# Two attention layers on one core: v in quarter products within the stream of q, k and projection

## The chip, the core and the metric

The kernel runs on one NeuronCore of a Trainium2 chip. Its time is the time of one execution on the device in microseconds (us), taken as the median of several runs. A profile of one further execution shows when each engine was busy and what it waited for. The engines are TensorE (PE, its weight loads are listed as PEld), VectorE (DVE), ScalarE (ACT), GpSimd (POOL) and SyncE (SP), which issues most transfers.

## The reference

Two layers of the same form are applied to x of 8 images, 512 channels and 32 x 32 positions, all in float32. They differ in the groups of the normalisation (8 and 32).

```python
xn = group_norm(x) * scale + bias                # (B, 512, 1024)
q, k, v = split(qkv_w @ xn + qkv_b)              # 8 heads of 64 channels each
attn = softmax(q^T k / 8)                        # (B, 8, 1024, 1024)
out = proj_w @ (v attn^T) + proj_b + x
```

## The kernel before

The work is cut into 16 units, one for each layer and image (`units`, L103). A unit has two stages on TensorE: the products of v, q and k, with the projection of the unit before it, and then the attention. All engines run the order that is written out in the code; waits between them are semaphores.

**Products by Strassen's scheme.** Every 512 x 512 by 512 x 1024 product is made of seven half-size products in Winograd's form. The weights' mixtures are made once, kept in DRAM as images (`store_image`, `load_image`, L186 to L194) and loaded for each unit. The mixtures of the activations are made in each unit by subtractions: class `Right` (L196) has `mix` (L215) for the outer level and `quarter` (L221) for the inner one. q, k and the projection use two levels: 7 x 7 parts. v uses one level.

**The stream** (`Stream`, L396). `product` (L407) makes one outer product of seven inner parts, one matmul with 256 columns each (L417), in the order 1, 6, 2, 7, 5, 4, 3 (`ORDER`, L50). Part 1 goes to `one`, a corner of one PSUM pair (`sbank`), and ACT copies it (`seed`, L422) to a quarter of another pair (`apair`), where later parts add to it; part 6 is then added to `one`, and so on. The seventh part goes to a corner of its own and is copied to `late` (L434). The last two parts, 4 and 3, stand in `tail` and run after part 1 of the following product, so that the copies of ACT lie beside matmuls. `finish` reads the finished pair with DVE (`sum_steps`, L456, and its users), and POOL adds `late` (`add_late`, L452). Consecutive products use the two pairs `apair` in turn. `hook` calls after each product what `at` has put there: pieces of other work in the order in which the engines shall do them.

**v** (`make_values`, L606). Each of the seven outer products is eight matmuls of 256 columns (L394), with the activations as weights, so that v comes out with positions on partitions. ACT copies two results, DVE adds five. In this time POOL makes the inner factors of x for q and k (`make_rooms`, `part_of`, L935 to L955, shown as L947), in rooms that lie in the tiles of k, of p and of tmp.

**The attention** (`attention`, L693). It has 64 steps, in 8 chunks of 8. A step makes scores (L718) in a PSUM pair, ACT takes the exponential into a tile p (L726; there are five such buffers), TensorE multiplies it with v (L746), and DVE adds p to a running sum (`summed`, L763 and L765). At the end of a chunk the result is evacuated (`evacuate`, L767: ACT copies one bank to tmp, DVE adds the other, L772), the sums are transposed and reduced (L777, L785), and some steps later `reciprocals` and `divide` (L796, L823) finish a pair of heads. `at_step` (L1081) puts the next unit's work in between: normalisation, two mixtures of x (L1116, by L217), loads of weights. The last pair's `reciprocals`, `divide` and `bias_last` are done in the next unit's hooks (L1017 to L1019), and the factors of its projection are made there by DVE (`o_rooms`, L1003, shown as L1015).

## Time and profile before

| what | value |
|---|---|
| median of 3 runs | 3210.49 us (3210.27 to 3212.94) |
| profiled execution | 3212.51 us |
| its span in the profile | 3210.7 us |
| granted TensorE clock | 0.999 |
| busy: PE, DVE, ACT, POOL | 3195.5, 2773.0, 1892.3, 930.4 us |
| one period: attention of unit 13; v, then q, k and projection, of unit 14 | 110.26; 24.71; 63.50 us |
| matmul records of v, L394, 128 x 256 (mean of one) | 382 ns |
| matmul records of the stream, L417, 128 x 256 | 379 to 386 ns |

The span runs from the first to the last instruction of the profile; the execution's own time has 1.8 us more around it. Busy times of an engine are of its instructions, and an idle engine costs nothing unless another waits for it. A matmul's record lasts longer than the step to the next one, because matmuls are pipelined: what counts is the distance from start to start. A float32 matmul gives two records. In the rows of the timeline, the first number is the start and the second the length in us; rows of like instructions in succession are merged, with their number at the end.

### The profile page before, as it was taken

The numbers are of one execution on the slowest core, as the hardware profiler recorded it, in microseconds if no ns is written. First come the engines' busy times: TensorE is split into PE (matmuls) and PEld (weight loads), VectorE is DVE, ScalarE is ACT, GpSimd is POOL, SyncE is SP. The second block draws the span as 40 slices with busy tenths as digits, with TensorE's granted clock in tenths as the row PEclk, the third lists the DMA queues.
The fourth block names the chain that finished last, engine by engine and source line by source line (L and its number), as shares of the span: only waits on it lengthen the run. The fifth ranks groups of instructions, "written<-read, shape, count | busy, mean of one in ns | idle before, by whom it ended". The sixth has DMA issues, their size and how long they took to land.

```text
span 3210.7 us, 59813 instructions
## 1 busy us (share of the span) xinstructions
PE 3195.5 (100%) x23012; PEld 2023.7 (63%) x23012; DVE 2773.0 (86%) x3315; ACT 1892.3 (59%) x3077; POOL 930.4 (29%) x619
## 2 busy tenths in 40 slices
PE   9999999999999999999999999999999999999999
PEld 7466584765847658476584755747557485674843
DVE  7988988989899898888988889898888988989877
ACT  3656746466465665746657465574655746557464
POOL 5133060330604306043150421504224042240520
PEclk9999999999999999999999999999999999999999
DMA  5334242442534314233142332423323233232311
GB/s 197 109 108 131 79 159 96 132 131 93 160 105 128 120 45 157 74 108 127 43 162 68 107 124 61 143 70 122 108 79 126 74 119 106 86 130 74 123 64 49
DMA packets 151361, 344.84 MB, mean 107 GB/s; under 512 B 27168, under 2 KB 40992, under 8 KB 151072
## 3 DMA queue, kind: packets, MB, share of 16 engines
q1 hardware_dynamic: 150784, 340.81, 33.2%
q8 instruction: 187, 3.06, 0.4%
q14 instruction: 102, 0.84, 0.1%
q10 hardware_dynamic: 288, 0.13, 0.0%
HBM read 282.29 MB, written 57.02 MB: 106 GB/s over the span
## 4 chain that ended last, share of the span: by engine, by line
PE 94%; DVE 3%; issue 1%; POOL 0%; ACT 0%; DMA 0%; SPq 0%; DVEq 0%; POOLq 0%; ACTq 0%
PE a L746 26%; PE s L718 25%; PE s L417 18%; PE a L417 13%; PE a L394 6%; PE s L394 5%; DVE acc L765 1%; PE a L718 1%; PE s L672 0%; PE a L672 0%; DVE tr L777 0%; DVE acc L763 0%; DVE red L785 0%; DVE ao L772 0%; DVE xt L217 0%
## 5 line engine op out<-in xcount | busy, mean ns | idle before, releaser
L726 ACT ACTIVATE p<-s 128x1024 f32<-128x1024 f32 x976 | 997.6, 1024 | 522.7 <-PE s L718 495.4
L746 PE MATMUL a<-p,v 64*64 64x512 f32 x8192 | 1102.3, 589 | 0.0
L718 PE MATMUL s<-q,k 64*64 64x512 f32 x7808 | 1060.8, 590 | 0.0
L765 DVE TENSOR_TENSOR acc<-acc,p 128x1024 f32<-128x1024 f32 x768 | 938.3, 1222 | 77.9 <-ACT p L726 34.6
L746 PEld LDWEIGHTS a<-p,v 64*64 64x64 f32 x8192 | 385.1, 132 | 494.2 <-ACT p L726 348.3
L718 PEld LDWEIGHTS s<-q,k 64*64 64x64 f32 x7808 | 388.1, 133 | 426.9 <-issue 426.9
L422 ACT COPY a<-s 128x256 f32<-128x256 f32 x1308 | 465.8, 357 | 282.3 <-PE s L417 202.4
L947 POOL TENSOR_TENSOR k<-xn 128x512 f32<-128x512 f32 x16 | 20.3, 1269 | 1337.0 <-DVE xn L217 1337.0
L434 ACT COPY late<-s 128x256 f32<-128x256 f32 x327 | 121.7, 372 | 179.9 <-PE s L417 178.8
L394 PE MATMUL a<-w,xn 128*128 128x256 f32 x768 | 178.2, 382 | 0.5 <-DVE v L623 0.5
L832 ACT ACTIVATE ao<-ao,vec 128x512 f32<-128x512 f32 x128 | 88.4, 715 | 143.9 <-DVE ao L825 143.7
L394 PEld LDWEIGHTS a<-w,xn 128*128 128x128 f32 x768 | 144.6, 190 | 31.8 <-issue 12.2
L763 DVE TENSOR_TENSOR acc<-p,p 128x1024 f32<-128x1024 f32 x128 | 152.5, 1192 | 9.4 <-ACT p L726 9.4
L777 DVE STREAM_TRANSPOSE tr<-acc 128x1024 f32<-128x1024 f32 x128 | 158.0, 1235 | 0.0
L785 DVE TENSOR_REDUCE red<-tr 128x32 f32<-128x1024 f32 x128 | 154.3, 1206 | 0.6
L417 PE MATMUL s<-xn,w 128*128 128x256 f32 x492 | 146.8, 380 | 1.2 <-POOL xn L947 1.2
L417 PE MATMUL s<-k,w 128*128 128x256 f32 x492 | 146.4, 379 | 0.0
L417 PE MATMUL a<-xn,w 128*128 128x256 f32 x492 | 146.4, 379 | 0.0
L772 DVE TENSOR_TENSOR ao<-a,tmp 128x512 f32<-128x512 f32 x128 | 88.1, 688 | 61.4 <-ACT tmp L771 61.2
L417 PE MATMUL a<-xt,w 128*128 128x256 f32 x462 | 137.5, 379 | 0.0
L288 POOL TENSOR_TENSOR y<-var,half 128x4 f32<-128x4 f32 (+1 forms) x17 | 22.8, 1340 | 381.7 <-DVE var L286 381.7
L417 PE MATMUL s<-xt,w 128*128 128x256 f32 x432 | 128.5, 379 | 0.0
(204 smaller groups left out, 4685.9 us busy)
## 6 DMA issues: line engine op xcount, KB each, us to landing
w<-iq SPq DMA_DIRECT2D x105, 448.0 KB, 3.4
w<-ik SPq DMA_DIRECT2D x105, 448.0 KB, 5.8
w<-io SPq DMA_DIRECT2D x105, 448.0 KB, 3.4
rb<-drec SPq DMA_DIRECT2D x128, 256.0 KB, 3.9
w<-iv SPq DMA_DIRECT2D x105, 256.0 KB, 2.8
xn<-mid SPq DMA_DIRECT2D x36, 512.0 KB, 3.5
xn<-x_dram SPq DMA_DIRECT2D x32, 512.0 KB, 4.3
res<-x_dram SPq DMA_DIRECT2D x32, 512.0 KB, 6.5
```

Source lines behind the costliest of these rows:

```text
L394: step()
L417: nc.tensor.matmul(dst, a[j], b[j], start=start, stop=j != 1, skip_group_check=True),
L422: n = nc.scalar.copy(dst, one)
L434: on("ACT", nc.scalar.copy(late, seventh), s, 1)
L718: nc.tensor.matmul(bank[e * H : (e + 1) * H, j, :], w.k[pr][j * H : (j + 1) * H, t * P + e * H : t * P + (e + 1) * H], w.q[pr][j * H : (j ...
L726: exp = nc.scalar.activation(p, bank, AF.Exp, scale=SCALE)
L746: nc.tensor.matmul(banks[r][j * H : (j + 1) * H, :], w.v[rows, t, lo : lo + D], p[rows, j, :], start=(t == 0), stop=(t == NT - 1),)
L763: nc.vector.tensor_add(acc, state["first"], p)
L765: nc.vector.tensor_add(acc, acc, p)
L777: nc.vector.transpose(tr, state["acc"].pop(c))
L785: nc.vector.tensor_reduce(red[:, :, qh, :], state["tr"].rearrange("p j (f i) -> p j f i", i=BL), AX.X, ALU.add)
L832: nc.scalar.activation(cols, cols, AF.Identity, bias=vec[:, units[u][0], VB, pr : pr + 1])
```

## The change

v is now made in two levels, too, except in unit 0: `stream_values` runs seven stream products before those of q. A part of v is two matmuls of 128 columns, with 128 positions of the activations as weights; the image of v's weights therefore has the inner mixtures too (448 KB for a product instead of 256). The results of v are added by DVE (p1's first half is copied by ACT), and POOL adds `late` to them.

The inner factors of x have to be there when v begins. A new method, `single`, makes those of one outer factor. The factors of products 1 and 6 are made by DVE in the attention before (`mixing`, steps 44 to 60), in rooms of k's first tile, and the two outer mixtures that were at steps 50 and 59 are at 43 and 50. The factors of products 2 and 3 are made by POOL at the end of the attention (`begin_high`: four subtractions of 128 x 512, in the buffers of p that come free next); those of 5, 7 and 4 by POOL after them, in rooms of k.

At the end of the attention, the last chunk is evacuated by DVE alone, a copy and an addition, ahead of its last sum; its transposition and reduction, and the bias of the pair before, go to hooks in v. The reciprocals and the division move to the ends of v and of q's second product. Of the projection's factors, DVE makes those of products 1, 5, 6 and 7, POOL those of 2, 3 and 4. The pairs of PSUM banks swap their parts from unit to unit (`banks_of`), since the stream now has 28 products. The check of the sums is done once, at the end, on maxima and minima kept for each pair of heads.

```diff
+    q_pairs, k_pairs = (
+        [qkpool.tile([P, 2, N], F32, tag=f"{sel}{r}", name=f"{sel}{r}") for r in range(2)] for sel in "qk"
+    )
...
-        def quarter(self, pair, rooms, engine):
+        def quarter(self, pair, rooms, engine, kept=None):
             v = self.views[pair[0]]
             t1, t2, t4 = rooms
             b11, b12, b21, b22 = (v[:, :, c, q, :] for c in range(2) for q in range(2))
+            b7 = b12 if kept is None else kept
...
+        def single(self, k, rooms, engine, kept=None):
+
+            v, (t1, t2, t4) = self.outer[k], rooms
+            b11, b12, b21, b22 = (v[:, c, q * FD2 : (q + 1) * FD2] for c in range(2) for q in range(2))
+            b7 = b12 if kept is None else kept
+            self.inner[k] = {1: b11, 2: b21, 3: b22, 7: b7, 5: t1, 6: t2, 4: t4}
+            sub = engine.tensor_sub
+            return [
+                partial(sub, t1, b12, b11), partial(sub, t2, b22, t1), partial(sub, t4, b21, t2),
+                partial(sub, b7, b22, b12),
             ]
...
             def part(j, dst, tile_name, bank, start=False):
-                on(
-                    "PE",
-                    nc.tensor.matmul(dst, a[j], b[j], start=start, stop=j != 1, skip_group_check=True),
-                    tile_name, bank,
-                )
+                for to, at, moving in (
+                    [(dst[:, ts(i, P)], b[j][:, ts(i, P)], a[j]) for i in range(2)]
+                    if tokens else [(dst, a[j], b[j])]
+                ):
+                    on(
+                        "PE",
+                        nc.tensor.matmul(
+                            to, at, moving, start=start, stop=j != 1, skip_group_check=True
+                        ),
+                        tile_name, bank,
+                    )
+                    start = False
...
+        cols = to[:, 1].rearrange("p (a t) o -> p a t o", a=2)
+        parts = late.rearrange("p (t o) -> p t o", o=P)[:, None].to_broadcast([P, 2, 2, P])
+        return nc.gpsimd.tensor_add(cols, cols, parts)
...
+            if bias is None:
+                on("ACT", nc.scalar.copy(t[:, 0, :], main[:, 0, :]), m, 0)
+                on("DVE", nc.vector.tensor_add(in_two(t[:, 1, :]), in_two(main[:, 1, :]), twice(late)), m, 1)
+                return
...
+    def stream_values(stream, w, left, hook):
+        st, p1, u2, u3, wide = sum_steps(None, None, f"v_{w.u}")
+
+        def block(r, h):
+            return w.v[:, ts(h, NT // 2), ts(r, FD2)].rearrange("p t (r o) -> p r t o", o=P)
+
+        def result(r, h, more):
+            def finish(main, m, late):
+                to = block(r, h)
+                w.last["v"].append(
+                    on("DVE", nc.vector.tensor_add(to, by_rows(main), by_rows(st[more])), m, 0, 1)
+                )
+                w.last["v"].append(add_late_v(to, late))
+
+            return finish
+
+        def fifth(main, m, late):
+            to = block(1, 1)
+            for i in range(2):
+                wide(main, m, i)
+                w.last["v"].append(
+                    on(
+                        "DVE",
+                        nc.vector.tensor_add(to[:, i], by_rows(main)[:, i], by_rows(st["u3"])[:, i]),
+                        m, i,
+                    )
+                )
+            w.last["v"].append(add_late_v(to, late))
+
+        steps = {
+            1: p1, 6: u2, 2: result(0, 0, "p1"), 7: u3, 5: fifth, 4: result(1, 0, "u3"),
+            3: result(0, 1, "u2"),
+        }
+        for k in ORDER:
+
+            def finish(main, m, late, k=k):
+                steps[k](main, m, late)
+                hook("v", k)
+
+            stream.product(left.quarters(k), w.right.inner[k], k == 3, finish, True)
...
+        def banks_of(c):
+            pair = (c + g) % 2
+            return abank[2 * pair : 2 * pair + 2]
...
-            i0 = nc.scalar.copy(tmp, banks[0])
+            if c == n_chunks - 1 and not final:
+                i0 = nc.vector.tensor_copy(tmp, banks[0])
+            else:
+                i0 = nc.scalar.copy(tmp, banks[0])
...
-            summed(s, p)
+            if s < n_steps - 1:
+                summed(s, p)
             at_step(s, state)
         products(n_steps - 1)
         evacuate(n_chunks - 1)
-        for h in range(NH):
-            add_bias(CC - 2, h)
-        transposed(n_chunks - 1)
-        reduced(n_chunks - 1)
+        summed(n_steps - 1, p)
+        w.sums = [partial(transposed, n_chunks - 1), partial(reduced, n_chunks - 1)]
...
+            right.mix(3)
+            fifth = right.single(5, in_k((1, 1, 3), (1, 0, 0), (1, 0, 1)), nc.gpsimd)
+            run(fifth[:2])
+            run(right.single(7, in_k((1, 0, 2), (1, 0, 3), (1, 1, 2)), nc.gpsimd))
+            run(fifth[2:])
+            at("v", 6, partial(right.mix, 2), partial(run, right.single(4, in_k((1, 1, 0), (1, 1, 1), (0, 1, 3)), nc.gpsimd)))
...
+            def o_rooms(ro=ro, parts=o_parts):
+                ta, tb = (trpool.tile([P, 2, FD], F32, tag="tr", name=f"o{i}_{u}") for i in "ab")
+                oa, ob = (ppool.tile([P, 2, FD], F32, tag="p", name=f"o{i}_{u}") for i in "cd")
+                v, g = nc.vector, nc.gpsimd
+                parts[1] = ro.single(1, [alone(ta, *i) for i in ((0, 0), (0, 1), (1, 0))], v)
+                parts[7] = ro.single(7, [alone(ta, 1, 1), alone(tb, 0, 0), alone(tb, 1, 0)], v)
+                parts[5] = ro.quarter((5, 6), (halves(tb)[1], *halves(oa)), v)
+                parts[2] = ro.quarter((2, 3), (*halves(ob), halves(xt[:, 1])[0]), g)
+                rooms = alone(xt[:, 1], 0, 1), alone(xt[:, 1], 1, 1), alone(xt[:, 0], 0, 0)
+                parts[4] = ro.single(4, rooms, g)
+
+            def o_part(k, lo=0, hi=4):
+                return lambda: run(o_parts[k][lo:hi])
+
+            transposed, reduced = old.sums
+            at("v", 1, transposed)
+            at("v", 2, reduced)
+            at("v", 4, reciprocals, old.bias_before)
+            at("v", 3, partial(ro.mix, 0), o_rooms)
+            at("q", 1, o_part(1, 0, 2))
+            at("q", 6, divide)
+            at("q", 2, bias_last, o_part(1, 2))
+            at("q", 7, partial(ro.mix, 1))
+            at("q", 4, partial(ro.mix, 3))
+            at("q", 3, partial(ro.mix, 2))
+            at("k", 1, o_part(5, 0, 2))
+            at("k", 6, o_part(5, 2))
+            at("k", 2, o_part(7), o_part(2, 0, 2))
+            at("k", 7, o_part(2, 2))
+            at("k", 4, o_part(4))
+
+        stream = Stream((u + 1) % 2)
+        if u == 0:
+            stream.close(
+                make_values(w, lefts["v"], (apair[1], sbank[0], apair[0]), hook, between, behind)
+            )
+        else:
+            stream_values(stream, w, lefts["v"], hook)
...
+        mixing = {}
+        if not last:
+            first_1 = right.single(1, [alone(w.kp[0], *at) for at in ((0, 0), (0, 1), (1, 0))], nc.vector)
+            first_6 = right.single(
+                6, [alone(w.kp[0], *at) for at in ((1, 1), (0, 2), (1, 2))], nc.vector, alone(w.kp[0], 0, 3)
+            )
+            mixing.update(zip((44, 46, 47, 52), first_1))
+            mixing.update(zip((54, 55, 59, 60), first_6))
+            mixing[43] = partial(right.mix, 0)
+            mixing[50] = partial(right.mix, 1)
+
+            def begin_high(right=right):
+                xa, xb = (ppool.tile([P, 2, FD], F32, tag="p", name=f"x{i}_{u + 1}") for i in "ab")
+                run(right.quarter((2, 3), (*halves(xa), halves(xb)[0]), nc.gpsimd, halves(xb)[1]))
...
+            if s in mixing:
+                mixing[s]()
 
         stream.close()
         attention(w, at_step)
+        if not last:
+            begin_high()
```

## The prediction

> **What bounds the kernel now.** I read the engine totals first, then one late period by stage, then the order in time of each engine around the one seam that the change rebuilds.
>
> ```profile
> PE 3195.5 (100%) x23012; PEld 2023.7 (63%) x23012; DVE 2773.0 (86%) x3315; ACT 1892.3 (59%) x3077; POOL 930.4 (29%) x619
> ```
>
> TensorE is busy all the time. The stage windows of one period say that this is real. The rows are the attention of unit 13 (2669.97 to 2780.23), and of unit 14 v (to 2804.94) and q, k and projection (to 2868.44):
>
> ```profile
> 2669.97:2780.23 110.26, 110.26 (x1034) 49.96 (x1033) 98.90 (x123) 76.27 (x83) 4.10 (x4) 1.00 0.25 77
> 2780.23:2804.94 24.71, 24.71 (x117) 21.73 (x115) 20.00 (x21) 5.53 (x8) 17.38 (x12) 1.00 0.36 127
> 2804.94:2868.44 63.50, 63.48 (x294) 55.17 (x293) 53.50 (x61) 37.37 (x104) 37.00 (x25) 1.00 0.42 136
> ```
>
> The columns after the length are busy time of PE, weight loads, DVE, ACT and POOL. PE has no hole in 198.47 us. DVE is busy for 98.9 of 110.3 us of the attention, so it has little room there. The timeline of PE gives the pace of the matmuls; each float32 matmul is two records:
>
> ```profile
> 12.41 1.39 PE L330 MATMUL s<-gmat 128*128 128x128 f32 x11
> 2777.48 2.81 PE L746 MATMUL a<-p,v 64*64 64x512 f32 x24
> 2780.23 3.72 PE L394 MATMUL a<-w,xn 128*128 128x256 f32 x16
> 2810.12 0.59 PE L417 MATMUL a<-k,w 128*128 128x256 f32 x2
> 2810.55 0.60 PE L417 MATMUL a<-xt,w 128*128 128x256 f32 x2
> ```
>
> A record of 256 columns starts every 0.216 us (2810.12 to 2810.55 is two), in v as in the stream. At the start of the program there is a row of 128 columns, each record with its own weight load: the 11 take 1.39 us and the last outlives its start by 0.28, so they start every (1.39 - 0.28) / 10 = 0.111 us; single records of it stand 0.112 apart. I use 0.112.
>
> The end of the attention on DVE, and ACT's copy at the start of the stream:
>
> ```profile
> 2775.43 1.22 DVE L217 TENSOR_TENSOR xt<-xn,xt 128x1024 f32<-128x1024 f32 x1
> 2776.56 1.22 DVE L765 TENSOR_TENSOR acc<-acc,p 128x1024 f32<-128x1024 f32 x1
> 2777.70 1.22 DVE L825 SCALAR_TENSOR_TENSOR ao<-ao,rb 128x1024 f32<-128x1024 f32 x1
> 2778.84 3.88 DVE L765 TENSOR_TENSOR acc<-acc,p 128x1024 f32<-128x1024 f32 x3
> 2782.64 0.68 DVE L772 TENSOR_TENSOR ao<-a,tmp 128x512 f32<-128x512 f32 x1
> 2804.33 0.36 ACT L422 COPY a<-s 128x256 f32<-128x256 f32 x1 [2.12 <-PE s L417]
> ```
>
> PE is through with the attention at T = 2780.23, DVE not before T + 3.1: it is 3 us late and has no hole. Now that costs nothing, because v's first products use the other pair of banks.
>
> **What the skill says.** The Trainium skill, "SBUF — State Buffer", section "Who interferes with whom": a VectorE instruction with two SBUF inputs and a GpSimd instruction that reads SBUF exclude each other for the whole instruction. The trace agrees:
>
> ```profile
> 2815.41 0.68 DVE L1015 TENSOR_TENSOR oa<-ot 128x512 f32<-128x512 f32 x1
> 2816.13 1.64 DVE L1015 TENSOR_TENSOR oa<-ot,oa 128x512 f32<-128x512 f32 x1
> 2815.58 1.64 POOL L454 TENSOR_TENSOR q<-q,late 128x512 f32<-128x512 f32 x1 [0.86 <-DVE q L510]
> ```
>
> POOL's sum comes during the first DVE operation and waits for it; the second DVE operation waits for POOL, 1.64 instead of 0.68 us. So they take turns, and one POOL operation on 128x512 costs DVE 0.96 us here, 1.07 at 2819.61. I use 1.0. In "TensorE: Matmul & The Clock Gate", section "Step-by-step", the weights of the next matmul load while this one runs; the 0.111 us above agrees, for a load that is itself recorded as 0.19 us.
>
> **The change, part by part.** The unit of account is one of the units 1 to 15; v of unit 0 stays as it was.
>
> (1) v's matmuls. Before: 7 products x 8 matmuls x 2 records = 112 x 0.216 = 24.19 us. After: 49 parts x 2 matmuls x 2 records = 196 x 0.112 = 21.95. That is -2.24, all on the path. A part takes 0.447 us.
>
> (2) The first product of the stream has no predecessor whose last parts could stand between its part 1 and part 6. Part 6 writes the bank that ACT's copy of part 1 reads. Part 1 ends at 0.61 (0.447 and 0.16 of pipeline); in the row above the copy starts 0.10 after such an end and takes 0.36; with a handoff of 0.1 back, part 6 starts at 1.15 instead of 0.45. +0.7.
>
> (3) The evacuation of the attention's last chunk. The second product accumulates in the pair of banks that this chunk filled, and its first copy waits for the evacuating addition on DVE. Part 6 of that product comes 8 parts after T: 0.7 + 8 x 0.447 = T + 4.28. Copy and handoffs take 0.56, so DVE has to be done by T + 3.72. When is it? Before, the sum of step 59 ends at 2775.51 = T - 4.72. In the sixth chunk three subtractions of 128x256 (0.35 each; 0.42 recorded, 0.34 apart) come in, the shorter reciprocals give back 0.36, and 0.19 goes into the gap between two sums that follow each other: T - 4.2. Then, in the new order: subtraction 0.34, sum 1.14, subtraction 0.34, division 1.14, sums 1.14 and 1.33, copy 0.60, addition 0.68, together 6.7: T + 2.5, in time. But begin_high puts four POOL operations on 128x512 at just this place: the first waits only for the sum of step 59, whose buffer it takes. Each takes its turn between DVE's, 4 x 1.0, and of the next one (128x256) half a hold, 0.25, on the average gets in: T + 6.7, rounded down to 6.6 for a sum that would have waited anyway. 6.6 - 3.72 = +2.9 on PE. Behind that copy on ACT wait the copies that end the first product; nothing else is late by then.
>
> (4) What I cost at nothing, and its cover. POOL's work by the end of v: 4 subtractions of 128x512 at 1.27, 12 of 128x256 at 0.77 and six late sums at 1.3 are 22 us in 25: PE's wait of (3) covers them; without it the factors are late (second rival). DVE after (3): in v five operations more (about 3.3 us in 20.0 of 24.7), in q, k and projection 3.5 us of factors fewer, which POOL makes in its 37.0 of 63.5 us. ACT: 35 copies of 0.36 more in v, where it has 5.5 of 24.7 us. DMA: 105 loads of v's image 192 KB larger, 20 MB, with the DMA engines under half busy in every window above. SP's order: the sums' small transfers and the row of reciprocals move to the end of v; DVE divides 6.7 us after them, about what it has now (2793.2 to 2799.6). The k images behind them on SP wait for the end of v anyway. Unit 0 and the end: some instructions reordered, 2 us either way.
>
> Sum: -2.24 + 0.7 + 2.9 = +1.36, times 15 = **+20.4 us**. The profiled execution took 3212.51 (span 3210.7 and 1.8 around it), so 3232.9 against it; the median of the runs is 2.0 lower, so 3231.
>
> **Bounds of what the trace doesn't show.** The 128-column pace with waits on semaphores: not below 0.107, half of 0.216 less a little; upward the recorded load of 0.19 would be paid in full. I take 0.112 because every record of that row loads weights. The wait of (3): from 0 (DVE a little less late, or POOL later) to 4.4 (full 1.27 per POOL operation and DVE 0.5 us later). (2): 0.5 to 0.9.
>
> **The rivals.** *Faster:* the evacuation is done in time. For it: without POOL it would be, with 1.2 us to spare. Against: the operands show that each of POOL's four and of DVE's six in that stretch needs the shared ports. Then -2.24 + 0.7 = -1.54, times 15 = -23: 3187. It decides from an addition that ends before T + 3.72; break-even is T + 5.26, as PE may lose 1.54 there.
> *POOL late instead:* DVE keeps the ports from operation to operation. Then POOL starts its four at T + 1.4 and with the sums and mixes of DVE in between has the second factor of product 7 at about T + 13.1, where PE wants it at 0.7 + 22 x 0.447 = T + 10.5; the last one 0.6 later still. -2.24 + 0.7 + 3.2 = +1.7: 3235, nearly the forecast's time. The same ports are short in either order.
> *Weight loads show:* 0.19 per record: 196 x 0.19 = 37.2, +13 per unit: 3405. Against it is the row of 0.111.
> *The clock:* the skill's clock-gate page (Part 1) has TensorE drop to half after an idle window of about 3.4 us; a wait of 3 us or more, 15 times, could touch that. No run here shows it (granted clock 1.00). I estimate from the page up to 1.7 us per unit: 3256.
>
> **How the numbers follow.** Forecast 0.50; POOL late 0.18; clock 0.08; weight loads 0.04; faster 0.20. About 6.4 us, 0.2%, is what a measurement of this kernel tells from no change. Of the forecast and of POOL late some 0.11 lies within it (a wait of 1.1 to 2.0), of faster 0.01: slower 0.69, same 0.12, faster 0.19. The forecast's own range is 3214 to 3254 (waits of 1.8 to 4.4). The range of 8 in 10 takes in half of the faster case and most of the clock case: 3187 to 3256.
>
> **What would show it.** 128x128 records 0.112 apart in v; PE idle some 0.7 us before the second part of v, and about 3 us before part 6 of v's second product, released by ACT's copy, which DVE's addition released; DVE sums of 2.2 us instead of 1.22 at the end of each attention beside POOL rows. No hole there, or one at product 7 put down to POOL, proves (3) wrong; a unit shorter than 198.47 us proves the sign wrong.

## The result, and the profile after

The changed kernel takes **3338.15 us** (median of 4, 3337.03 to 3342.84) against 3211.5 us: ratio **1.0397** (95% interval 1.0379 to 1.0415). The prediction was 3231, with a range up to 3256. The sign was right; the size, +20 us, was a sixth of the +127 us measured. The profiled execution took 3342.84 us, its span is 3341.0.

The engine totals of the changed kernel, from its page:

```profile
PE 3211.3 (96%) x24272; PEld 2070.1 (62%) x24272; DVE 2805.4 (84%) x3344; ACT 2043.4 (61%) x3572; POOL 1139.2 (34%) x833
```

PE was busy for 100% of the span and is now for 96%: some 130 us of holes. The windows of the same period as before (attention of unit 13; v; q, k and projection of unit 14) say where:

```profile
2787.24:2897.48 110.24, 110.24 (x1034) 49.75 (x1033) 100.54 (x121) 76.28 (x83) 7.24 (x6) 1.00 0.28 90
2897.48:2926.63 29.15, 24.79 (x200) 24.17 (x199) 22.71 (x26) 14.38 (x39) 21.08 (x20) 0.94 0.01 2
2926.63:2992.30 65.67, 63.97 (x294) 54.96 (x292) 50.13 (x60) 38.46 (x107) 43.41 (x29) 1.00 0.51 179
```

The attention is as long as before. v takes 29.15 us and not 24.71, and PE is busy for 24.79 of them at a granted clock of 0.94; q, k and projection take 65.67, 2.2 more, where the prediction had nothing. Below, T is the end of the attention (2897.48), and a wait is what the distance between two starts of matmul records has over 0.112 us (128 columns) or 0.216 (256).

The pace of v, from PE's timeline: four records in 0.44 us, as predicted.

```profile
2922.13 0.61 PE L435 MATMUL a<-w,k 128*128 128x128 f32 x4
2922.57 0.61 PE L435 MATMUL a<-w,xt 128*128 128x128 f32 x4
```

The seam, from the timeline of DVE, POOL and ACT:

```profile
2893.74 0.42 DVE L1234 TENSOR_TENSOR k<-xt,k 128x256 f32<-128x256 f32 x1
2894.07 2.32 DVE L848 TENSOR_TENSOR acc<-acc,p 128x1024 f32<-128x1024 f32 x1
2895.39 2.13 POOL L408 TENSOR_TENSOR xa<-xn,xa 128x512 f32<-128x512 f32 x1
...
2897.72 2.28 DVE L906 SCALAR_TENSOR_TENSOR ao<-ao,rb 128x1024 f32<-128x1024 f32 x1
...
2899.94 3.94 DVE L848 TENSOR_TENSOR acc<-acc,p 128x1024 f32<-128x1024 f32 x2
...
2901.10 1.70 POOL L408 TENSOR_TENSOR k<-xt 128x256 f32<-128x256 f32 x1
2902.88 1.58 POOL L408 TENSOR_TENSOR k<-xt,k 128x256 f32<-128x256 f32 x1
2903.80 0.68 DVE L855 COPY tmp<-a 128x512 f32<-128x512 f32 x1
2904.52 0.69 DVE L858 TENSOR_TENSOR ao<-a,tmp 128x512 f32<-128x512 f32 x1
...
2905.30 0.63 ACT L443 COPY a<-s 128x256 f32<-128x256 f32 x2 [4.10 <-DVE ao L858]
```

DVE's sum and its division take 2.3 us beside POOL and not 1.22. The evacuating addition ends at T + 7.7, and ACT's copy, which PE needs for part 6 of v's second product, has waited 4.10 us for it. PE's wait there is 3.8 to 5.1 us in units 6 to 15, 3.9 in unit 1, and 6.5 in units 2 to 5; in most units another 0.26 us is lost between the first two records behind it. What the prediction gave a chance of 0.08 follows: the clock. The next two windows, 3.5 and 3.4 us long, begin where PE goes on; the third number from the end is the clock. In the first of them matmul records start 0.213 us apart, twice the 0.112.

```profile
2905.60:2909.10 3.50, 3.39 (x16) 3.40 (x17) 3.50 (x4) 1.64 (x5) 1.46 (x2) 0.51 0.00 0
2909.10:2912.50 3.40, 3.40 (x32) 3.40 (x32) 1.86 (x3) 1.80 (x5) 3.20 (x5) 1.00 0.00 0
```

Three more waits were in none of the steps. In k, DVE's four subtractions for the projection's product 7 and POOL's for its products 2 and 3 come from one hook, the end of k's product 2:

```profile
2959.71 1.38 DVE L408 TENSOR_TENSOR ob<-ao,oa 128x256 f32<-128x256 f32 x1
2960.76 1.45 POOL L408 TENSOR_TENSOR od<-ao 128x512 f32<-128x512 f32 x1
2961.12 1.37 DVE L408 TENSOR_TENSOR ob<-ao,ob 128x256 f32<-128x256 f32 x1
...
2963.82 1.40 DVE L518 SCALAR_TENSOR_TENSOR u_k<-a,step_vec,u_k 128x512 f32<-128x512 f32 x2
2964.65 0.63 ACT L443 COPY a<-s 128x256 f32<-128x256 f32 x2 [1.88 <-DVE u_k L518]
```

DVE operations of 0.41 us take 1.4 and k's sum is late: PE waits 1.55 us in every unit. Twice in a unit, at the ends of v's product 4 and of q's product 2, ACT does two bias operations in a row ahead of a copy that PE waits for (0.40 and 0.46 us). Here the first of the two:

```profile
2923.10 1.33 ACT L913 ACTIVATE ao<-ao,vec 128x512 f32<-128x512 f32 x2
...
2924.34 0.37 ACT L443 COPY a<-s 128x256 f32<-128x256 f32 x1
...
2924.76 0.71 PE L435 MATMUL s<-w,xa 128*128 128x128 f32 x4 [0.23 <-ACT a L443]
```

And in unit 0, DVE waits for the projection's raw weights, with k's sums and PE (10.6 us) behind it:

```profile
74.06 8.16 SPq L169 DMA_DIRECT2D w<-proj_wT_dram  x4
...
87.73 1.42 DVE L408 TENSOR_TENSOR w<-w 128x512 f32<-128x512 f32 x2 [12.32 <-DMA w<-proj_wT_dram]
```

The whole, in starts of the stages: v of unit 1 begins at 210.17 us and not at 195.91 (+14.3); the other 15 units add the rest, 209.15 us a period from the attentions of units 1 to 4 on (199.49 before) and 205.53 from those of units 5 to 14 on (198.48 before).

### The profile page after: what moved, and what is told of

It is laid out like the page before. It is cut to its first block, busy times and chain, and to the rows that moved or that the text cites. A ratio compares the mean times of both kernels' runs of the same rounds, so it can differ in the third digit from the quotient of the medians.

```text
span 3341.0 us, 63709 instructions
## 1 busy us (share of the span) xinstructions
PE 3211.3 (96%) x24272; PEld 2070.1 (62%) x24272; DVE 2805.4 (84%) x3344; ACT 2043.4 (61%) x3572; POOL 1139.2 (34%) x833
## 4 chain that ended last, share of the span: by engine, by line
PE 71%; DVE 20%; issue 4%; ACT 3%; DMA 1%; SPq 1%; DVEq 0%; ACTq 0%
PE s L435 22%; PE s L801 16%; PE a L829 16%; PE a L435 16%; DVE acc L848 10%; DVE acc L846 2%; DVE tr L863 2%; DVE ao L906 1%; DVE ao L858 1%; DMA lt<-red 1%; ACT ao L913 1%; PE a L801 1%; SPq L877 1%; ACT a L443 1%; DVE red L871 1%
## 5 line engine op out<-in xcount | busy, mean ns | idle before, releaser
L848 DVE TENSOR_TENSOR acc<-acc,p 128x1024 f32<-128x1024 f32 x768 | 974.9, 1269 | 71.1 <-ACT p L809 35.6
L443 ACT COPY a<-s 128x256 f32<-128x256 f32 x1728 | 614.6, 357 | 472.0 <-PE s L435 264.8
L408 POOL TENSOR_TENSOR xa<-xn 128x512 f32<-128x512 f32 x15 | 19.1, 1275 | 1187.9 <-PE a L829 536.3
L455 ACT COPY late<-s 128x256 f32<-128x256 f32 x432 | 160.7, 372 | 232.8 <-PE s L435 231.2
L435 PE MATMUL s<-k,w 128*128 128x256 f32 x672 | 198.2, 384 | 25.3 <-ACT a L443 25.2
L435 PE MATMUL s<-w,k 128*128 128x128 f32 x660 | 119.2, 316 | 75.5 <-ACT a L443 75.5
L435 PEld LDWEIGHTS s<-k,w 128*128 128x128 f32 x672 | 123.9, 190 | 52.7 <-ACT a L443 37.7
L435 PEld LDWEIGHTS s<-w,k 128*128 128x128 f32 x660 | 102.7, 226 | 81.2 <-ACT a L443 81.2
L475 POOL TENSOR_TENSOR q<-q,late 128x512 f32<-128x512 f32 x64 | 111.8, 1748 | 63.8 <-DVE q L546 32.6
L484 POOL TENSOR_TENSOR v<-v,late 128x512 f32<-128x512 f32 x60 | 89.9, 1498 | 89.6 <-ACT a L443 46.0
```

The lines of the kernel that those rows point to most:

```text
L435: nc.tensor.matmul(to, at, moving, start=start, stop=j != 1, skip_group_check=True),
L443: n = nc.scalar.copy(dst, one)
L455: on("ACT", nc.scalar.copy(late, seventh), s, 1)
L475: return nc.gpsimd.tensor_add(cols, cols, twice(late))
L848: nc.vector.tensor_add(acc, acc, p)
```

## The experiments

All start from the changed kernel. Ratios are to the kernel before, measured again beside each run. The last two columns are mean periods (the attention of a unit with the products that follow it, so v of unit 2 falls into the period of unit 1); "late units" are 5 to 14. In the kernel before these are 199.49 and 198.48 us.

| run | us | ratio (95%) | units 1-4 | late units |
|---|---|---|---|---|
| changed kernel | 3338.15 | 1.0397 (1.0379-1.0415) | 209.15 | 205.53 |
| e1 | 3329.19 | 1.0364 (1.0347-1.0381) | 209.00 | 205.13 |
| e2 | 3295.80 | 1.0261 (1.0244-1.0278) | 206.70 | 202.29 |
| e3 | see text | | 204.23 | 200.07 |
| e4 | 3400.00 | 1.0583 (1.0566-1.0601) | 212.46 | 209.83 |
| e5 | 3323.94 | 1.0348 (1.0331-1.0365) | 207.47 | 204.65 |
| e6 | 3316.89 | 1.0326 (1.0309-1.0343) | 207.89 | 203.69 |
| e7 | 3249.54 | 1.0114 (1.0097-1.0131) | 202.87 | 200.59 |
| e9 | 3229.41 | 1.0059 (1.0042-1.0075) | 201.20 | 199.26 |
| e10 | 3229.86 | 1.0057 (1.0040-1.0074) | 201.25 | 199.27 |
| e11 | 3230.23 | 1.0057 (1.0043-1.0071) | 202.29 | 198.89 |
| e12 | 3234.87 | 1.0074 (1.0061-1.0088) | 201.22 | 199.74 |
| e13 | 3345.38 | 1.0414 (1.0400-1.0428) | 208.09 | 207.16 |
| e14 | 3221.65 | 1.0035 (1.0023-1.0048) | 199.76 | 199.14 |
| e15 | 3267.78 | 1.0177 (1.0163-1.0191) | 202.73 | 202.12 |
| e16 | 3213.07 | 1.0006 (1.0000-1.0013) | 199.17 | 198.41 |
| e17 | 3232.59 | 1.0068 (1.0054-1.0082) | 200.50 | 200.04 |
| **e18** | **3196.17** | **0.9950 (0.9937-0.9964)** | 197.13 | 197.43 |

### Each cause by itself: e1 to e6

**e1**, unit 0: the raw weights first.

```diff
-            at("q", 3, partial(run, inner_k[3:]), partial(store_image, 0, "k", left_first_k))
+            at(
+                "q", 3, partial(run, inner_k[3:]), partial(load_raw, 0, "o", slot_q),
+                partial(store_image, 0, "k", left_first_k),
+            )
...
-            at("q", 3, partial(store_image, 0, "v", slot_v), partial(load_raw, 0, "o", slot_q))
+            at("q", 3, partial(store_image, 0, "v", slot_v))
```

> Only unit 0 is changed: the raw weights of the projection are loaded ahead of the stores of k's and v's images, not behind them. Theory (transfer late): in the changed kernel DVE waits 12.3 us for these weights in k's second product of unit 0, and k's sums behind that wait hold PE for about 10.6 us, after which the granted clock is at half for 13.65 us. With the loads ahead, the wait and the half clock go, and v of unit 1 starts near 196 to 198 us of the span and not at 210.2: 12 to 14 us less, about 3325. Rival (the tile is free too late: it holds q's weights until q's last product at 70 us, and 1 MB has still to come): a wait of 3 to 6 us stays, 6 us less, about 3332. Later units: nothing.

v of unit 1 starts at 197.83 us: 12.3 of the 14.3 us are back, and the wait and its half clock are gone. The median falls by 9.0, the profiled execution by 17.5; in these two executions the half clock behind v's wait took 28.1 us in all with e1 and 30.8 without. Of the other executions there is no trace, so where 3 us of the median went stays open. The load was late because it stood in SP's order behind the stores of two images, one of which (v's, with its inner mixtures) the change had put there.

**e2**, on DVE the evacuation ahead of the last sums.

```diff
-            if c % NH == 1 and t == 5 and c > 1:
+            if c % NH == 1 and t == 5 and c > 1 and (final or s < n_steps - NT):
                 divide(c // NH - 1)
...
-            if s < n_steps - 1:
+            if s < n_steps - (1 if final else 3):
                 summed(s, p)
...
         evacuate(n_chunks - 1)
-        summed(n_steps - 1, p)
+        for s in range(n_steps - (1 if final else 3), n_steps):
+            summed(s, state["p"][s])
+        if not final:
+            divide(CC - 2)
```

> The evacuation of the last chunk stands on DVE ahead of the sums of steps 61 and 62 and of the division of the third pair, which come after it. POOL's four subtractions stay where they are. Theory A (DVE and POOL take turns at the end of the attention, and the evacuation queues behind the sums that this makes long): the evacuating addition ends near T + 1.5 to 3.9, PE's wait before part 6 of v's second product falls from 4.05 (6.7 in units 2 to 5) to 0.5 or less (1 in units 2 to 5), the half clock behind it goes; some 85 to 105 us less, 3233 to 3253, less what the delayed sum of the first product costs at the third (up to 1 us in a unit, 15 us). Theory B (the sums behind are needed at once elsewhere): the wait moves to v's third product with the same length, within 20 us of 3338.

The addition ends at T + 1.65, and the wait of 4 us is gone; in units 2 to 5 0.4 of it stays. But 42 us come back and not 85 to 105: DVE's sum of v's first product now stands behind the deferred sums, and PE waits 1.6 us (3.8 in units 2 to 5) at the third product, and 0.7 to 1.0 at the fourth. Theory A holds for the first wait; about half of what it freed turned into the next waits for DVE.

**e3**, the four POOL operations left out.

```diff
-                xa, xb = (ppool.tile([P, 2, FD], F32, tag="p", name=f"x{i}_{u + 1}") for i in "ab")
-                run(right.quarter((2, 3), (*halves(xa), halves(xb)[0]), nc.gpsimd, halves(xb)[1]))
+                b11, b12, b21, b22 = (right.views[2][:, :, c, q, :] for c in range(2) for q in range(2))
+                right.quarter((2, 3), (b11, b21, b22), nc.gpsimd)
```

`quarter` only names the quarters here; the subtractions that it returns are not run.

> POOL's four subtractions of 128x512 at the end of the attention are left out; the unsubtracted quarters stand in for the factors of v's, q's and k's products 2 and 3, so these products are computed from other data. The order on DVE is that of the changed kernel. Theory A (shared ports): DVE's last sums take 1.22 us again instead of 2.2 but where the two POOL operations on 128x256 that follow meet them, the addition ends by about T + 4, the wait is 0.5 or less and the half clock goes: 3233 to 3250. Theory B (DVE is late by its own added operations, the ports do little): a wait of at least 2 us stays, 3290 or more.

The stand-in factors take the softmax's sums out of their bounds, so the kernel runs its second, general path as well (10701 us in all); what counts is the trace of the units. The same place, at the end of unit 13's attention (T = 2827.29):

```profile
2823.88 1.22 DVE L848 TENSOR_TENSOR acc<-acc,p 128x1024 f32<-128x1024 f32 x1
...
2825.89 1.75 DVE L906 SCALAR_TENSOR_TENSOR ao<-ao,rb 128x1024 f32<-128x1024 f32 x1
...
2827.57 2.54 DVE L848 TENSOR_TENSOR acc<-acc,p 128x1024 f32<-128x1024 f32 x2
2830.03 0.68 DVE L855 COPY tmp<-a 128x512 f32<-128x512 f32 x1
2830.74 0.69 DVE L858 TENSOR_TENSOR ao<-a,tmp 128x512 f32<-128x512 f32 x1
```

The sums take 1.22 us, the addition ends at T + 4.1 and the wait is 0.2 to 0.6 us outside units 2 to 5. Same order on DVE, none of the four POOL operations: so POOL's turns are the cause, theory A. (Step (3) had T + 2.5 for this case. DVE begins 0.46 us later than it said, and POOL's next two operations, on 128x256, now come here and cost 1.1 us.) In units 2 to 5, 2.7 us stay: there DVE is late by itself, through the mixing of the next layer's weights in the attention.

**e4** and **e6**, sixteen products into the wait. This is the edit of e6; e4 has the same matmul without `on(...)`, which tells the program that only one bank of the pair is meant.

```diff
             self.close()
+            for _ in range(idle):
+                on(
+                    "PE",
+                    nc.tensor.matmul(
+                        sbank[i][:, 1, FD2 : FD2 + P], b[6][:, :P], a[6], start=True, stop=True,
+                        skip_group_check=True,
+                    ),
+                    f"s{i}", 1,
+                )
             part(6, one, s, 0)
...
+            stream.product(left.quarters(k), w.right.inner[k], k == 3, finish, True, 16 if k == 6 else 0)
```

> Sixteen products of 128 columns (3.6 us at full clock) that nobody reads are put into PE's order ahead of part 6 of v's second product, where PE waits 3.8 to 6.5 us. They fill the wait and don't make it longer. Theory C (the half clock for 3.4 us or more after it comes from PE standing idle): the granted clock stays at full through v, the remaining wait is 0.4 (3 in units 2 to 5): 1.7 us less in each of the eleven late units and 3.4 in units 2 to 5, 32 us in all, 3306. Theory D (the half clock is a limit on the matmuls with 128 columns and would come anyway): the clock falls as before, 3338 or a little more.

In e4 they lacked `on(...)` and so waited for the whole bank pair, that is, for the same ACT copies as part 6: the wait stayed (4.05 us or more), the products came after it, the first of them at half clock, and the run tells nothing of C and D.

> The sixteen idle products again, now held only by the copy of the seventh part of v's first product, which ACT makes before the late copy; in the run before they waited for the same copy as part 6 and so came after the wait. Theory C (the half clock comes from PE standing idle for the 3.8 us or more): PE runs through the wait, the clock stays at full, 1.7 us less in eleven units and up to 3.4 in units 2 to 5, 3306. Theory D (the half clock belongs to the products of 128 columns): the clock falls as before, 3338 or somewhat more.

Here they ran in the wait. The window of v of unit 14, with 0.7 us of q behind it (the last number but two is the clock):

```profile
2872.01:2900.60 28.59, 27.50 (x236) 26.80 (x235) 23.46 (x27) 14.56 (x40) 21.48 (x20) 1.00 0.01 3
```

Theory C: with PE busy the clock stays at 1.00. Summed over the records that start at double distance, less the same sum in the kernel before, the half clock costs 30.8 us in the changed kernel and 9.8 here. Of these, 4 and 6 us are single records: the second one behind a wait starts late in every unit. The rest here comes from units 2 to 5, where 2.9 us of waiting are left, and three of these four waits are still followed by the half clock. The median falls by 21.3.

**e5**, POOL's projection factors one product later.

```diff
-            at("k", 2, o_part(7), o_part(2, 0, 2))
-            at("k", 7, o_part(2, 2))
-            at("k", 4, o_part(4))
+            at("k", 2, o_part(7))
+            at("k", 7, o_part(2, 0, 2))
+            at("k", 4, o_part(2, 2))
+            at("k", 3, o_part(4))
```

> Only the places of POOL's projection factors are changed: products 2 and 3 go to the ends of k's products 7 and 4 and product 4 to the end of k's product 3, one product later than in the changed kernel, so that DVE's four subtractions for product 7, at the end of k's product 2, have no POOL operation beside them. Theory A (the wait of 1.55 us at the sixth product of k comes from these two taking turns): the 1.55 goes in every unit but the first, 23 us less, 3315. Theory B (DVE has too much in k in any case, or POOL's operations meet k's sums elsewhere): a wait of like length comes up one or two products later, 3330 to 3340.

The 1.55 us are gone in all units and nothing comes up in k: theory A. Yet the median falls by 14.2 and not 23. The same sum of half-clock records is 38.9 us here against 30.8: with v's wait unchanged the clock stayed down longer behind it (over 5 us in most late units, 2.8 to 3.4 in most before). I have no run that says why; e5 also ran on another chip than e1 to e4, and nothing here separates the two.

### Repairing all: e7 to e18

**e7**: e1, e5, and at the seam: evacuation, `mix(3)`, sums 61 to 63, division on DVE; POOL makes product 2's factors singly, then 7, 5, 4, 3.

```diff
-                run(right.quarter((2, 3), (*halves(xa), halves(xb)[0]), nc.gpsimd, halves(xb)[1]))
+                run(right.single(2, rooms, nc.gpsimd, alone(xa, 1, 1)))
...
+                run(right.single(3, rooms, nc.gpsimd, alone(xb, 1, 1)))
+
+            at("v", 2, make_third)
```

> All the repairs together: the projection's raw weights first in unit 0; on DVE the evacuation, then the mixture for product 7, then the sums of steps 61 to 63 and the third pair's division; POOL makes the factors of product 2 alone at the end of the attention, in four subtractions of 128x256, then those of 7, 5, 4, and those of 3 at the end of v's second product; POOL's factors for the projection one product later in k, DVE's second pair for product 1 at the end of q's first product, and the bias of the third pair in two halves at the ends of v's products 4 and 3. Theory A (v costs -2.24 + 0.97 a unit, and everything else was order and not lack of time): every wait but the first one of v, 0.97, goes; unit 0 stays 2 us longer; 3212.5 + 2 - 15 x 1.27 = 3195, up to 3205 with small remainders. Theory B (POOL and DVE have more to do at this seam than fits into it in any order): waits of 1.3 us or more in v's products 2 to 7 in every unit, 3215 to 3240.

88.6 us of the 127 are back. The waits left (1.05, 0.69, 0.95 and 0.46 in a late unit) are those that the next text names. The 0.46 in q had been put down by me to DVE; it stayed when DVE's operation was moved, and went when ACT's two bias operations were separated (e9).

**e9** (DVE: one sum, then the sum of v's first product, then the rest) and **e10** (part 7 of v's first product ahead of part 6). The edit of e10 begins with `early`.

```diff
+            at("v", 1, *old.behind[1:], transposed)
+            at("v", 6, old.divide_before)
...
+            early = tokens and self.tail is None
+            if early:
+                part(7, seventh, s, 1, not keep)
             self.close()
             part(6, one, s, 0)
...
```

> The run with all the repairs still had four waits of PE in each unit: 1.05 us at v's third product and 0.69 at its fourth (DVE's sum of the first product stands behind the deferred sums and the division, and the next sum behind it), 0.95 at its last (POOL's late sum of the fourth product stands behind the factors of product 3) and 0.46 in q (two bias operations of 0.64 us together on ACT). Here DVE does only the sum of step 61 before the sum of the first product, those of 62 and 63 and the transposition after it, and the division after the sixth; POOL makes two of the factors of product 3 after v's second product and two after its late sum for product 7; the bias of the last pair is done in two halves. Theory A (order, not lack of time): the four waits go, 3.1 us a unit, 47 us less: 3203, and below the kernel before. Theory B (the seam is full): half or more of it comes back in other places, 3225 to 3250.

> As the run before, and in v's first product part 7 comes ahead of part 6, into the time in which PE waits for ACT's copy of part 1. Theory: this wait, 0.67 of the 0.97 us that v's first product loses, is mostly the missing work between part 1 and part 6; a part of 0.447 us put there takes 0.45 us off in each unit, 6.7 us in all, 3196 if the run before comes to 3203. Rival: the copies on ACT only shift (the copy of the seventh part comes between the copies that PE waits for): no difference to the run before, within 2 us.

e9 gets 20 of its 47 us; 0.66, 0.94 and 0.53 us came up at later products, as theory B says of it. e10 turns the wait of 0.67 into two of 0.22, each with a late second record behind it. So it frees 0.12 us a unit and not 0.45, and in units 2 to 5 the fourth product, which waits for DVE, takes that back (1.60 us for 1.47). The time is the same.

**e11**: the mixtures and subtractions for x earlier in the attention, the evacuating copy on ACT.

```diff
-            mixing.update(zip((44, 46, 47, 52), first_1))
-            mixing.update(zip((54, 55, 59, 60), first_6))
+            mixing.update(zip((35, 36, 38, 40) if u else (41, 42, 44, 45), first_1))
+            mixing.update(zip((49, 50, 52, 54), first_6))
...
+            mixing[56] = partial(right.mix, 3)
```

> The run before still lost 2.1 us a unit where DVE's sums in v come late (0.66 at the fourth product, 0.94 at the fifth) and where POOL's factors of product 3 do (0.53). Here 3 us of DVE's work leave the seam: the mixtures for products 5, 6 and 7 and the eight subtractions for 1 and 6 are spread over steps 33 to 56 of the attention and not 43 to 60 and v's beginning, the copy of the last evacuation is made by ACT, and the division of the third pair comes after v's fourth product. Theory A (DVE's time at the seam is the limit, and the attention still has room for some of it): the waits fall to 0.7 or less in sum, a unit to 197.6 or less against the 198.47 of the kernel before, 3195 to 3204, faster than before. Theory B (the attention is full as well): DVE reaches the end of the attention later by what was added, the evacuation waits again, 3225 to 3250.

The time does not change; of the two theories both hold in part: late units from 199.27 to 198.89, but the attentions of units 1 to 4 grow to 113 us, since DVE mixes weights there too.

**e12**: the weights' mixing over units 1 to 8. This is no part of the change.

```diff
-    MAKE = {1: (1, "v"), 2: (1, "q"), 3: (1, "k"), 4: (1, "o")}
+    MAKE = {2 * i + j + 1: (1, sel, j) for i, sel in enumerate("vqko") for j in range(2)}
...
+            at("v", 4, old.divide_before)
+            at("v", 3, reciprocals, partial(ro.mix, 0), o_rooms, partial(old.bias_before, 0))
```

> The run before came to 198.4 to 199.3 us a unit from unit 6 on, as the kernel before, but lost 3.6 us in each of units 1 to 4 (their attentions were 113 us long: the mixing of the next layer's weights is on DVE as well) and let DVE stand idle for 1.8 us ahead of the sum of v's first product. Here the mixing of the weights is spread over eight units, four operations in each (with the half-mixed weights taken back from their image), the sums of steps 61 and 62 come before that sum again, the third pair's division after v's sixth product and the reciprocals after its last, and in the units without weights to mix the mixture for product 4 is made in the attention. Theory A (order and spreading are enough; DVE has the room over the whole period): units at 197.2 to 198, 3190 to 3208. Theory B (DVE and POOL have no more room together than the kernel before uses): units stay at 198.5 to 199.5, 3212 to 3228.

At 3234.87 a miss of both theories. v's waits fall to 0.44 at its first product and 0.3 to 1.5 at its last, but DVE's division in q now waits for the reciprocals' transfer, because I had moved these later: 1.36 us.

**e13** to **e18** move such remainders; each fault was one of order, seen in the trace and mended in a later run. Each edit is shown in part, against the run before it (e16 against e12); the expectations name the rest.

**e13**, the reciprocals earlier and the third pair's division later.

```diff
-            at("v", 4, old.divide_before)
-            at("v", 3, reciprocals, partial(ro.mix, 0), o_rooms, partial(old.bias_before, 0))
+            at("v", 4, reciprocals)
+            at("v", 3, old.divide_before, partial(ro.mix, 0), o_rooms, partial(old.bias_before, 0))
```

> In the run before PE had three kinds of waits left: 1.36 us in q (DVE's division of the last pair waits 1.84 us for the transfer of the reciprocals, which start too late), 0.3 to 1.5 at v's last product (POOL's factors of product 3) and 0.8 to 1.1 in the attentions of units 2, 4, 6 and 8 (the mixing of weights stands ahead of the normalisation's means). Here the reciprocals come after v's sixth product again and the third pair's division after its last, POOL makes the fourth factor of product 3 third and its late sum for v's second product after them, and the mixing stands at steps 19, 25, 31 and 37. Theory A (order alone): units from 9 on at 197.0 to 197.4, those with weights to mix at 197.5 to 198.5; 3195 to 3205, faster than the kernel before. Theory B (no room left on DVE and POOL): the waits come back elsewhere, units stay at 198.5 or more, 3212 to 3235.

A miss: the third pair is here divided by the last pair's reciprocals, so its result is not the one meant, and the division waits for them: 4.37 us on DVE, 6.7 or more on PE, then half clock. Up to that place there was no wait over 1 us.

**e14**, the division back ahead of the reciprocals.

```diff
-            at("v", 4, reciprocals)
-            at("v", 3, old.divide_before, partial(ro.mix, 0), o_rooms, partial(old.bias_before, 0))
+            at("v", 4, old.divide_before, reciprocals)
+            at("v", 3, partial(ro.mix, 0), o_rooms, partial(old.bias_before, 0))
```

> As the run before, with its fault mended: the third pair's division and then the last pair's reciprocals come together after v's sixth product, so that the division doesn't read the tile of the reciprocals that come later; the weight mixing stands at steps 17, 21, 25 and 29. The reciprocals start some 1.5 us earlier than in the run with the mixing spread out, in which DVE waited 1.84 us for their transfer in q. Theory A (order alone): q's wait falls from 1.36 us to 0.4 or less and v's last product waits 0.3 or less; units from 9 on at 197.0 to 197.5, those with weights to mix at 197.5 to 199; 3195 to 3207, faster than the kernel before. Theory B (no room on DVE and POOL): waits of 1.3 us or more a unit come up elsewhere, units at 198.5 or more, 3212 to 3235.

Half way: 3221.65. In most units 0.6 to 1.1 us of waiting are left late in v and 0.3 in q.

**e15**, the last pair's division and the bias of both pairs later in q.

```diff
-            at("q", 6, divide)
-            at("q", 2, partial(bias_last, 1))
+            at("q", 2, divide, partial(bias_last, 1))
...
-            at("q", 4, partial(ro.mix, 3))
+            at("q", 4, partial(ro.mix, 3), partial(old.bias_before, 0))
```

> As the run before, with POOL's late sum for v's second product back in its place, the division of the last pair one product later in q, the two halves of the third pair's bias in q and not at v's end, and the mixture for product 7 after the attention in units 2, 4, 6 and 8. No operation less on any engine. Theory A (order alone): units from 9 on at 197.2 to 197.7, units 1 to 8 at 197.5 to 199.5; 3196 to 3207, faster than the kernel before. Theory B (DVE and POOL have no room): waits of 1 us or more a unit come up elsewhere and the units stay at 198.4 or more, 3212 to 3225.

A miss, by ACT's order. From its timeline in q:

```profile
2258.91 1.22 DVE L907 SCALAR_TENSOR_TENSOR ao<-ao,rb 128x1024 f32<-128x1024 f32 x1
...
2260.16 0.72 ACT L914 ACTIVATE ao<-ao,vec 128x512 f32<-128x512 f32 x1 [2.49 <-DVE ao L907]
2260.79 0.36 ACT L443 COPY a<-s 128x256 f32<-128x256 f32 x1
...
2261.21 0.70 PE L435 MATMUL s<-k,w 128*128 128x256 f32 x2 [2.26 <-ACT a L443]
```

The bias waits for the division on DVE, and ACT's copies for PE wait behind the bias: 2.42 us in every unit.

**e16**, from e12 again: the division later, its bias one and two products behind it.

```diff
-            at("q", 6, divide)
-            at("q", 2, partial(bias_last, 1))
-            at("q", 7, partial(ro.mix, 1), partial(bias_last, 0))
+            at("q", 2, divide)
+            at("q", 7, partial(bias_last, 1))
+            at("q", 5, partial(ro.mix, 1), partial(bias_last, 0))
...
-                if t == 3 and c in range(1, 5):
+                if s in (17, 21, 25, 29):
```

> As the run with the weight mixing spread over eight units, with three moves: the last pair's division comes after q's second product (its reciprocals arrive 1.84 us too late for the sixth), its bias on ACT one and two products later, when the division is long done, and with it the mixture for product 6 of the projection; POOL makes the fourth factor of v's product 3 third; the mixing of weights stands at steps 17, 21, 25 and 29. Theory A (order alone): the 1.36 us in q and most of the 0.3 to 1.5 at v's last product go, units from 9 on at 197.0 to 197.5, units 1 to 8 at 197.5 to 199.5; 3196 to 3206, faster than the kernel before by 0.2% or more. Theory B (DVE and POOL have no room left): 1 us or more a unit comes back elsewhere, units at 198.4 or more, 3210 to 3225.

Level with the kernel before (21 runs). Units 9 and 12 take 197.05 and 196.92 us, the others from 10 on up to 198.3; units 1 to 8 mix weights now, and the attentions of 2, 4, 6 and 8 take 111.8 to 112.8.

**e17**, the mixing of weights earlier, and two of POOL's factors on DVE.

```diff
-                if s in (17, 21, 25, 29):
+                if s in (3, 5, 7, 18):
...
-                third.extend(right.single(3, rooms, nc.gpsimd, alone(xb, 1, 1)))
-                third[2:] = third[3], third[2]
+                third.extend(right.single(3, rooms, nc.gpsimd, alone(xb, 1, 1))[:2])
+                third.extend(right.single(3, rooms, nc.vector, alone(xb, 1, 1))[:1:-1])
```

> As the run before, with the mixing of weights at steps 3, 5, 7 and 18 of the attention, where DVE has no evacuation, transposition or reduction to do yet, and with two of the four factors of v's product 3 on DVE and not on POOL, after v's fourth product, where DVE waits 1.8 us for PE. Theory A (order and the sharing-out alone): units 2, 4, 6 and 8 fall by 1.5 to 2.5 us, v's last product waits 0.3 or less: about 8 + 9 us less, 3196 to 3205, faster than the kernel before. Theory B (the limit of DVE and POOL): as before or worse, 3210 to 3220.

The attentions of units 1 to 14 come to 110.26 to 110.44 us: theory A for the weights. The two factors on DVE come late and PE waits 1.9 to 3.3 us.

**e18**, these factors on POOL again.

```diff
-                third.extend(right.single(3, rooms, nc.gpsimd, alone(xb, 1, 1))[:2])
-                third.extend(right.single(3, rooms, nc.vector, alone(xb, 1, 1))[:1:-1])
+                third.extend(right.single(3, rooms, nc.gpsimd, alone(xb, 1, 1)))
+                third[2:] = third[3], third[2]
```

> As the run before, with all four factors of v's product 3 on POOL again. Theory A (order alone): the attentions of units 1 to 8 stay at 110.3 to 110.5, v's last product waits 0.9 at most, units at 197 to 198.3; against the run that was level with the kernel before (3213) it is some 9 us less, 3202 to 3207, faster than the kernel before by 0.15 to 0.3%. Theory B (the limit of DVE and POOL): the time won in the attentions comes back in v or q, 3210 to 3216.

**3196.17 us**: 0.5% faster than the kernel before (0.9950, 0.9937 to 0.9964), and 142 us below the changed one. So nearly all of the waits were order and not lack of time; the repairs also gave one copy of DVE to ACT and spread the mixing of weights. Its engine totals, and the same period as above:

```profile
PE 3172.1 (99%) x24272; PEld 2022.6 (63%) x24272; DVE 2704.3 (85%) x3329; ACT 2053.2 (64%) x3587; POOL 1125.9 (35%) x893
```

```profile
2652.73:2762.99 110.26, 110.26 (x1033) 49.88 (x1032) 99.82 (x123) 76.25 (x83) 4.10 (x4) 1.00 0.29 90
2762.99:2787.01 24.02, 23.28 (x201) 22.66 (x199) 17.86 (x17) 13.80 (x38) 23.29 (x25) 1.00 0.01 2
2787.01:2850.87 63.86, 63.66 (x295) 55.02 (x293) 48.89 (x67) 39.87 (x109) 43.63 (x30) 1.00 0.51 184
```

v takes 24.02 us in this unit, 0.7 less than before the change (24.71), and POOL is busy for 23.29 of them: hardly any room is left there. This period is one of the longer ones, with a wait of 0.79 us at v's last product; those without one take about 196.9, 1.6 less than before. Of the 18.8 us between its span (3191.9) and that of the kernel before, the periods of units 5 to 14 give 10.5 (1.05 each) and those of units 1 to 4 give 9.4; I estimate that 4 of these come from the spread-out weights, since in the kernel before these periods are 1.0 longer each than the late ones. Unit 0 takes 1.0 back and the end of the program 0.2.

## Why the prediction was wrong, step by step

Three things failed: the size of step (3), by 30 us; three of the terms that step (4) put at nothing, 55 us with the late records behind their waits; and the clock, 27 us, which was left to a rival of 0.08. Step by step:

**Step (1), right.** The records start 0.112 us apart. -2.24 a unit is there.

**Step (2), nearly right.** The wait is 0.67 us, and a record behind it starts 0.10 late: 0.77 for 0.7. (v's second record also starts 0.10 late, but did so before the change. The 0.97 in the expectations of e7 and e10 is 0.1 to 0.2 too much.)

**Step (3), the mechanism right, the term too small.** The addition ended at T + 7.7 and not T + 6.6. Nearly half of this is DVE's own: it began the stretch, with the subtraction at 2893.74, at T - 3.74 where the step had T - 4.2. From there the stretch took 11.5 us, of which 6.7 are the operations by themselves, as in the step, and 4.8 are POOL's turns, where the step had 4.25, rounded down to 4.15. So PE waited 3.8 us for 2.9. The same 11.5 us are in every unit; in unit 12 DVE began 1.3 us later and the wait was 5.1. In units 2 to 5 DVE began 2.7 us later and it was 6.5: the mixing of weights, which is in the code of `at_step`, was in no step. I had taken a late unit for all. Sum over 15 units: 74 us with the 0.26 behind the waits, where 44 were in the forecast.

**The clock, a rival of 0.08 that came true.** The Trainium skill, "TensorE: Matmul & The Clock Gate", Part 1, has the clock drop after an idle window of about 3.4 us; the forecast had 2.9 us of waiting and so kept it apart. The waits were longer: some 27 us of half clock in all, shown by e6 to be a consequence of PE standing idle. The rival's price of 1.7 a unit was right as the mean of the late units (1.3 to 2.6). But shorter waits brought the half clock too, and one of 3.33 us did not (last section): for this kernel the measured waits decide, not the length of the page's window.

**Step (4), wrong in three of its zeros.** *DVE and POOL in k*: 1.55 a unit, 23 us. The sums of busy time (POOL 37.0 of 63.5) said that there was room; that the two were given their work by the same hook was to be read in the code, and the turns at the ports were priced in this same text. *ACT*: two bias operations behind each other at the ends of v's product 4 and of q's product 2 cost 0.40 and 0.46, 13 us; busy time again. *Unit 0*: "2 us either way" was +14.3. I had not followed SP's order in unit 0, where the raw weights went from an early place behind the stores of two images.

Together, for the 15 units and unit 0, each wait with the late record behind it: matmuls -34; v's first product +12; evacuation +74; half clock +27 (the 30.8 without the single records); k +25; bias +16; unit 0 +14. That is 134. The kernel before had some 4 us of small waits that the changed one doesn't have (2.6 of them in v of units 3 to 5); with these taken off, the 130 us between the two spans are accounted for.

Of the rivals, "POOL late" and "weight loads" did not happen; POOL's late sums and factors show in the repaired versions only. "Faster", priced at -1.54 a unit, was within reach by order, but in many places: the units of e18 without a wait at v's last product gain 1.6, after all of the repairs.

## What to carry to other kernels

A seam between two stages is costed by writing out the order of each engine over it, SP's too, for the first unit and for the units with extra work as well, since busy shares say nothing on it. Operations that share ports are put where the other engine waits for something else; a hook that hands work to both at once makes both late. Where a wait of PE comes near 2 us, its price is not its length alone.

## What the hardware showed that I had not expected

- The clock fell after much shorter waits than in the forecast's picture. Of e15's 15 waits of 2.42 us, 7 were followed by records at double distance; of e17's seven of 1.9 to 2.0 us, one; of the waits of 1.55 us in the changed kernel none, of its fifteen of 3.8 us and over all. In between it was open: of e17's eight waits of 2.5 to 3.3 us seven were followed by it, but one of the two of 3.33 us was not. How long it lasts differs for like waits (2.8 to 5.5 us after waits of 3.8 to 4.2); no run here explains it.
- In turns with POOL operations on 128x512, DVE operations of 0.41 us on 128x256 took 1.4 us each and those of 1.22 us on 128x1024 took 2.3: a turn cost about 1 us whatever the length of the DVE operation, so short ones lost most.
